# Expert tiles taken in pairs: the last 48 hidden columns of two tiles turned together and multiplied on half of the array's rows each, with their weights fetched per tile

## The chip, the cores and the metric

The kernel runs on one core of one Trainium2 chip, as one launch. The time is the device time of that core in microseconds (us), taken as a median over runs; a profile is one execution of its own. Engines are named as the profile does: PE multiplies matrices (PEld is its loading of weights), DVE is the vector engine, ACT the scalar engine, POOL is GpSimd, and SP issues most transfers. Each engine works through its own list of instructions in order, and waits where one needs a result that is not there.

## The reference, cut to what matters

The input is x, 4 sequences of 1024 rows with 256 columns, all in float32. Four blocks follow, each added to x: an attention, a mixture of experts, a short convolution, and the same mixture of experts once more. The two mixtures are what the change is about:

```
shared_out = silu_and_mul(xf @ shared_w1.T) @ shared_w2.T      # hidden width 352
probs      = softmax(xf @ gate_w.T);  weights, selected = top_k(probs, 6)   # 16 experts
gate_up    = einsum('th,eoh->teo', xf, w1)                      # 2 x 176 columns per expert
act        = silu(gate) * up                                    # 176 columns
moe_out    = einsum('te,tei,ehi->th', combine, act, w2)         # 176 -> 256
```

The kernel computes only the six chosen experts of each row. An expert's hidden width is 176: one block of 128 and a rest of 48.

## The kernel before

All of x stays in on-chip memory as X. The 4096 rows are split in two groups of 2048 (16 blocks of 128 rows each). A mixture of experts over one group is a *stage*, so there are four: group 0 and group 1 of the first mixture, then group 0 and group 1 of the second. Rows are sorted by expert in DRAM: POOL scatters each normalized row to six slots of a queue `xq` (96 scatters of 128 rows each per stage, `scatter`, L397), the stage works through the queue in 111 tiles of 128 slots, all slots of a tile having one expert, writes the results to `yq`, and POOL gathers them back (96 gathers per stage, `combine`, L1121), where DVE adds them into X with their routing weight (L1131, one for each gather).

`stream` (L986) runs all 4 x 111 = 444 tiles in rounds. Round c issues, in this order on each engine:

- `load`: every third round, SP reads the rows of three tiles, six tiles ahead (L1001).
- `gate_up(c)` (L1018): PE loads the expert's number into a register and multiplies the turned rows by 352 columns of `wgu`, which holds the weights of all experts; ACT takes the silu and DVE multiplies (L1039) into `hbuf`.
- `turn_h(c-2)` (L1041): two PE transposes of the 256 columns of `hbuf` (176 are filled, the rest is zero), one ACT copy. DVE's product of a tile is thus needed two rounds later.
- `turn(c+2)`: two PE transposes of the input rows, one ACT copy.
- `down(c-3)` (L1049): the 128 rows `w2a`, then the rest `w2b`, padded with zeros to 128 rows; both hold all experts. ACT copies the result to `yo`; SP writes `yo` to `yq` for three tiles at once.
- the *callback* of tile c-3: one call of `bites.step`.

A float32 multiplication is two passes, so it shows as two PE instructions; a transpose shows as one.

The callbacks fit all other work between the tiles. It lies in three lanes of generators, cut by `yield` into pieces ("bites"), and `bites.step(pe, (q, s, f))` issues up to q, s and f bites of the lanes QUEUE, SIDE and FILL, of these at most `pe` with PE work. In the two middle stages (L1202):

- QUEUE first holds the gathers of the stage before (48 bites of two gathers; each bite also uses the gathers of an earlier bite, which DVE waits for), and later the scatters for the next stage (one bite of preparation, 48 of two scatters).
- SIDE: whenever the gathers have completed a quarter of the group (12 bites), a convolution (9 bites, nearly all DVE) and a preparation of the routing (6 bites: statistics, root on ACT, normalizing on DVE, then three with PE work, the first of which turns the normalized rows, tile `fpt`) are added. After the last quarter comes `plan` (14 bites, mostly DVE), which sorts the rows. The scatters are added to QUEUE once SIDE is empty.
- FILL: the shared expert (`shared`, L930), one bite after every fourth tile.

If the scatters are not all issued when round 109 of a stage needs the first row of the next, `force` issues the rest there, and PE waits for them (`turn`). The first stage (`first`) has QUEUE scatters for stage 1 only, the last one (`final`) only gathers. After the last tile there remain the gathers of group 1, with the shared expert of group 1 between them.

The order on PE, DVE, ACT and SP is exactly that of the program.

Of the kernel before, what the change touches and what calls it, by code (L numbers as in the profile page):

```python
# [15 lines left out]
PE = mybir.EngineType.PE  # L16

# [20 lines left out]
FB = FI - P  # L38
VW = D + 1
# [64 lines left out]
def block_kernel(  # L104
# [193 lines left out]
    def plan(g, ps):  # L298
# [80 lines left out]
        for c in range(0, NTILE, 37):  # L379
            yield "el"  # L380
            le = rt.tile([1, 37, NEXP], FP, name="le")
            sh_le = [1, 37, NEXP]
            nc.vector.tensor_tensor(
                le,
                base[:, None, :].to_broadcast(sh_le),
                row0[:, c : c + 37, None].to_broadcast(sh_le),
                ALU.is_le,
            )
            nc.vector.tensor_reduce(ex[:, c : c + 37], le, AX.X, ALU.add)
# [498 lines left out]
    with ExitStack() as fctx:  # L888
# [3 lines left out]
        f3 = fctx.enter_context(tc.tile_pool(name="f3", bufs=3))  # L892
        ps_t = fctx.enter_context(tc.tile_pool(name="ps_t", bufs=2, space=PSUM))
        ps_g = fctx.enter_context(tc.tile_pool(name="ps_g", bufs=2, space=PSUM))
        ps_y = fctx.enter_context(tc.tile_pool(name="ps_y", bufs=1, space=PSUM))
        ps_s = fctx.enter_context(tc.tile_pool(name="ps_sh", bufs=2, space=PSUM))
        ps_m2 = fctx.enter_context(tc.tile_pool(name="ps_m2", bufs=1, space=PSUM))

        def ps_f():
            return ps_m2  # L900
# [14 lines left out]

        w2r = w2.rearrange("(n i) e -> i n e", i=FI)
        w2a = fw.tile([P, NEXP, E], FP, name="w2a")
        nc.scalar.dma_start(out=w2a, in_=w2r[0:P])
        w2b = fw.tile([P, NEXP, E], FP, name="w2b")
        nc.vector.memset(w2b[32:64], 0.0)  # L920
        nc.vector.memset(w2b[64:P], 0.0)
        nc.scalar.dma_start(out=w2b[0:FB], in_=w2r[P:FI])
        wgu_f = [wgu[:, k].rearrange("p n f -> p (n f)") for k in range(2)]
        w2_f = [w.rearrange("p n e -> p (n e)") for w in (w2a, w2b)]

        hbuf = [fw.tile([P, 2 * P], FP, name=f"hbuf{i}") for i in range(4)]
        for hb in hbuf:
            nc.vector.memset(hb[:, FI:], 0.0)

        def shared(g, i):  # L930
# [12 lines left out]
            for k in range(2):  # L943
                pt = ps_s.tile([P, 512], FP, tag="s", name="hpt")
# [3 lines left out]
            for s, rows in enumerate(S_ROWS):  # L948
                yield "pe"
                pg = ps_s.tile([P, 512], FP, tag="s", name="pg")  # L950
                pu = ps_s.tile([P, 512], FP, tag="s", name="pu")
# [14 lines left out]
            for pr in range(2):  # L966
                yield "pe"
                po = ps_s.tile([P, 2, E], FP, tag="s", name="po")
# [17 lines left out]
        def stream(stages):  # L986
# [5 lines left out]
            xg, xT, hT, yo, off = {}, {}, {}, {}, {}  # L992
# [24 lines left out]

            def gate_up(c):  # L1018
                st, i = tiles[c]
                _, vals = nc.values_load_multi_w_load_instructions(  # L1020
                    plan_of[st][2][0:1, i : i + 1],
                    engines=[PE],
                    min_val=0,
                    max_val=NEXP - 1,
                    skip_runtime_bounds_check_because="an expert's number",
                )
# [10 lines left out]
                h = hbuf[c % 4]  # L1037
                nc.scalar.activation(h[:, 0:FI], pg[:, 0:FI], AF.Silu)  # L1038
                nc.vector.tensor_mul(h[:, 0:FI], h[:, 0:FI], pg[:, FI:])  # L1039

            def turn_h(c):  # L1041
                pt = ps_t.tile([P, 2, P], FP, tag="t", name="pht")
                for k in range(2):
                    nc.tensor.transpose(pt[:, k, :], hbuf[c % 4][:, k * P : (k + 1) * P], ident)  # L1044
                hT[c] = f3.tile([P, 2, P], FP, name="hT")
                d = nc.scalar.copy(hT[c], pt)  # L1046
                pace["after"] = d.ins.name

            def down(c):  # L1049
                st, i = tiles[c]  # L1050
                py = ps_y.tile([P, E], FP, name="py")
                for k in range(2):
# [268 lines left out]
```

## Time and profile before

| what | us |
|---|---|
| median of 3 runs (lowest, highest) | 2390.59 (2389.18, 2391.22) |
| profiled execution, device time | 2393.24 |
| its span, first to last instruction | 2391.5 |
| PE busy | 2114.5 (88%) |
| DVE, ACT, POOL busy | 1118.5, 1240.2, 901.4 |
| attention, up to the first weights of the experts | about 765 |
| tiles of the four stages, with the waits between | 857 to 2260 |
| gathers and shared expert after the last tile | 2260 to 2391 |

The profile's page gives busy time per engine and 40 slices of the span; groups of instructions are named by line, engine and "out<-in"; a timeline merges instructions of one kind that follow each other (x4) and gives the start of the first. Starts are therefore what one measures with; the ends of PE's multiplications are modelled and overlap the next one's start.

### The profile page before, as it was taken

Reading aid. Unit: us, or ns where it says so; the run is one execution under the profiler, and the core shown is the slowest. Engines: PE = TensorE matmul, PEld = TensorE weight load, DVE = VectorE, ACT = ScalarE, POOL = GpSimd, SP = SyncE. Lnnn points to the kernel's source line nnn. Section 1 sums busy time; section 2 is a strip of 40 time slices with the busy share of each in tenths; the row PEclk is TensorE's granted clock in tenths of the full one; section 3 lists DMA queues with packets and bytes.
Section 4 is the critical chain, followed back from the end, with each engine's and each line's share of the span. In section 5 each row is a group of like instructions: output and inputs, shape, how many; then the busy total and the mean of one; then the engine's idle time right before and its main releaser. Section 6 shows DMA issues by size and latency. Waiting matters only on the chain.

```text
span 2391.5 us, 33033 instructions
## 1 busy us (share of the span) xinstructions
PE 2114.5 (88%) x10480; PEld 1308.4 (55%) x10480; DVE 1118.5 (47%) x2532; ACT 1240.2 (52%) x2754; POOL 901.4 (38%) x990
## 2 busy tenths in 40 slices
PE   5899999778898998999899999789999959999974
PEld 2344443222233466777666667567676747777632
DVE  5888867656555225111166652126754212441154
ACT  3677878566676145555455544335553424555410
POOL 3333211344431000444355226645513654540176
PEclk8888988889888999999999999989999979999987
DMA  7900000111101412555455335344423535663243
GB/s 232 342 7 1 1 1 1 38 51 45 53 27 62 114 48 79 165 166 166 137 151 154 102 104 176 132 139 142 145 92 121 176 124 154 202 186 115 91 123 112
DMA packets 212231, 267.73 MB, mean 112 GB/s; under 512 B 25280, under 2 KB 187232, under 8 KB 212064
## 3 DMA queue, kind: packets, MB, share of 16 engines
q1 hardware_dynamic: 166944, 161.04, 21.6%
q0 software_dynamic: 36992, 100.78, 13.4%
q10 hardware_dynamic: 8128, 3.80, 0.7%
q8 instruction: 91, 1.49, 0.3%
q14 instruction: 76, 0.62, 0.1%
HBM read 123.72 MB, written 141.82 MB: 111 GB/s over the span
## 4 chain that ended last, share of the span: by engine, by line
PE 67%; DVE 12%; issue 7%; ACT 7%; POOL 5%; DMA 2%; ACTq 0%; POOLq 0%; DVEq 0%; SPq 0%
PE pgu L1030 20%; PE py L1053 14%; PE ps L694 6%; PE acc L742 4%; PE pxt L1014 4%; PE pht L1044 4%; POOL xq L421 3%; PE pg L955 3%; ACT s L705 3%; PE pj L571 3%; PE pu L955 3%; PE po L972 3%; POOL yg L1147 2%; ACT s L863 1%; DVE X L1131 1%
## 5 line engine op out<-in xcount | busy, mean ns | idle before, releaser
L421 POOL DMA_INDIRECT xq<-sxn,sloti x384 | 379.2, 987 | 644.7 <-ACT xgT L1016 306.2
L1030 PE MATMUL pgu<-wgu,xgT 128*128 x1776 | 609.7, 466 | 4.4 <-DVE hbuf L1039 2.2
L1147 POOL DMA_INDIRECT yg<-yq,sloti x384 | 375.8, 979 | 421.8 <-issue 201.4
L1039 DVE TENSOR_TENSOR hbuf<-hbuf,pgu 128x176 f32<-128x176 f32 x444 | 149.4, 337 | 721.7 <-ACT hbuf L1038 721.2
L1030 PEld LDWEIGHTS pgu<-wgu,xgT 128*128 128x128 f32 x1776 | 338.7, 193 | 136.5 <-issue 20.3
L1038 ACT ACTIVATE hbuf<-pgu 128x176 f32<-128x176 f32 x444 | 141.4, 318 | 411.7 <-PE pgu L1030 411.6
L705 ACT ACTIVATE s<-ps 128x1024 f32<-128x1024 f32 (+3 forms) x384 | 291.4, 815 | 114.6 <-PE ps L694 113.5
L1053 PE MATMUL py<-w2a,hT 128*128 x888 | 268.7, 385 | 0.9 <-ACT yo L1062 0.9
L1053 PE MATMUL py<-w2b,hT 128*128 x888 | 266.4, 382 | 0.0
L1062 ACT COPY yo<-py 128x256 f32<-128x256 f32 x444 | 166.1, 374 | 167.0 <-PE py L1053 166.7
L1131 DVE SCALAR_TENSOR_TENSOR X<-yg,top,X 128x256 f32<-128x256 f32 x384 | 186.0, 484 | 87.8 <-DMA yg<-yq,sloti 81.8
L1014 PE MATMUL pxt<-ident,xg 128*128 128x128 f32 x888 | 171.8, 276 | 60.6 <-DMA xg<-xq 60.6
L714 POOL TENSOR_SCALAR_AFFINE_SELECT s<-s 128x256 f32<-128x256 f32 x128 | 84.2, 659 | 349.7 <-ACT s L705 349.5
L725 DVE TENSOR_TENSOR s<-s 128x1024 f32<-128x1024 f32 (+3 forms) x160 | 168.2, 1051 | 86.8 <-ACT s L705 83.5
L1016 ACT COPY xgT<-pxt 128x256 f32<-128x256 f32 x444 | 167.9, 378 | 68.7 <-PE pxt L1014 68.3
L694 PE MATMUL ps<-q,kA 32*128 32x512 f32 (+3 forms) x1024 | 182.0, 647 | 20.0 <-ACT s L705 18.0
L1044 PEld LDWEIGHTS pht<-ident,hbuf 128*128 128x128 f32 x888 | 125.9, 142 | 124.4 <-issue 71.1
L1053 PEld LDWEIGHTS py<-w2b,hT 128*128 128x128 f32 x888 | 170.2, 192 | 23.5
L863 ACT ACTIVATE s<-s 128x1024 f32<-128x1024 f32 x192 | 164.4, 856 | 27.5 <-POOL s L714 27.2
L1044 PE MATMUL pht<-ident,hbuf 128*128 128x128 f32 x888 | 171.6, 275 | 4.9 <-ACT hT L1046 4.9
L1046 ACT COPY hT<-pht 128x256 f32<-128x256 f32 x444 | 165.4, 372 | 1.7 <-PE pxt L1014 0.7
L742 PE MATMUL acc<-s,vA 128*32 128x512 f32 (+3 forms) x1024 | 140.1, 603 | 13.2 <-ACT s L863 10.8
(158 smaller groups left out, 2421.9 us busy)
## 6 DMA issues: line engine op xcount, KB each, us to landing
xg<-xq SPq DMA_DIRECT2D x148, 384.0 KB, 3.7
yq<-yo SPq DMA_DIRECT2D x148, 384.0 KB, 2.8
xq<-zero SPq DMA_DIRECT2D x74, 384.0 KB, 4.6
xq<-sxn,sloti POOLq DMA_INDIRECT x384, 2.4
yg<-yq,sloti POOLq DMA_INDIRECT x384, 2.9
wgu<-in_w SPq DMA_DIRECT2D x4, 1408.0 KB, 17.8
X<-in_x SPq DMA_DIRECT2D x8, 512.0 KB, 5.5
out<-X SPq DMA_DIRECT2D x8, 512.0 KB, 3.5
```

The lines of the kernel that those rows point to most:

```text
L421: d = nc.gpsimd.indirect_dma_start(out=xq[g][:, :], out_offset=bass.IndirectOffsetOnAxis(ap=sloti[:, c + i, k : k + 1], axis=0), in_=xs[:, ...
L694: nc.tensor.matmul(tiles[h // 2][:, h % 2, 0:nq], lhsT=kt[32 * h : 32 * h + 32, (j % 4) * P : (j % 4 + 1) * P], rhs=qT[u, hf][a][32 * h : ...
L705: nc.scalar.activation(s2[:, :, 0:nq], tiles[pr][:, :, 0:nq], AF.Square)
L725: nc.vector.tensor_mul(part, part, part)
L742: nc.tensor.matmul(acc[32 * r : 32 * r + 32, n0:512], lhsT=va[:, j % 4, h * VW : h * VW + 32], rhs=s2s[r // 2][:, r % 2, 0 : 512 - n0], st ...
L863: nc.scalar.activation(part, part, AF.Square)
L1014: nc.tensor.transpose(pt[:, k, :], xg[c][:, k * P : (k + 1) * P], ident)
L1030: nc.tensor.matmul(pg, lhsT=xT[c][:, k, :], rhs=wgu_f[k][:, bass.ds(vals[0] * (2 * FI), 2 * FI)], start=(k == 0), stop=(k == 1),)
L1044: nc.tensor.transpose(pt[:, k, :], hbuf[c % 4][:, k * P : (k + 1) * P], ident)
L1053: nc.tensor.matmul(py, lhsT=hT[c][:, k, :], rhs=w2_f[k][:, bass.ds(off[c] * E, E)], start=(k == 0), stop=(k == 1),)
L1131: nc.vector.scalar_tensor_tensor(X[:, t, l, :], yg[:, k, :], top[:, i, k0 + k : k0 + k + 1], X[:, t, l, :], op0=ALU.mult, op1=ALU.add,)
L1147: nc.gpsimd.indirect_dma_start(out=yg[:, k, :], out_offset=None, in_=yq[g][:, :], in_offset=bass.IndirectOffsetOnAxis(ap=sloti[:, i, k0 + ...
```

## The change

Tiles of a stage are taken in pairs (55 pairs and one single tile). The product of the even tile lies in the first 176 of 384 columns of an `hbuf`, that of the odd tile in the last 176; so the middle 128 columns hold the last 48 of the even tile, 32 zeros, and the first 48 of the odd one. `turn_h` turns the outer block of each tile, and the middle block once per pair. `down` runs once per pair: each tile's block of 128 against `w2a[0]` or `w2a[1]` (rows 0 to 127 and rows 48 to 175 of each expert), then the rest of each tile on 64 of the 128 rows of the array (rows 0 to 63 and 64 to 127), with 48 weight rows and 16 zero rows. These rest weights no longer lie on chip for all experts: in the round that turns a tile's input rows, two before its `gate_up`, SP loads the expert's number and fetches 48 KB into one of three buffers. Results are copied and written for two tiles at once.

The rest of the edit is in the fitting of other work: `plan` counts its table in pieces of 19, so in six bites where it had three; the middle stages take one and two bites of QUEUE in turn (they took one) and three of SIDE (they took two); the gathers of the last stage and after it come two to a bite, one bite after each tile, where they came three to a bite after every second tile; four gather buffers and three bites in flight where there were three and two; the shared expert and the preparation use one pool of two PSUM buffers, where the preparation had one of its own.

```diff
-        for c in range(0, NTILE, 37):
+        for c in range(0, NTILE, 19):
+            n = min(19, NTILE - c)
...
+        f4 = fctx.enter_context(tc.tile_pool(name="f4", bufs=4))
...
-        w2a = fw.tile([P, NEXP, E], FP, name="w2a")
-        nc.scalar.dma_start(out=w2a, in_=w2r[0:P])
-        w2b = fw.tile([P, NEXP, E], FP, name="w2b")
-        nc.vector.memset(w2b[32:64], 0.0)
-        nc.vector.memset(w2b[64:P], 0.0)
-        nc.scalar.dma_start(out=w2b[0:FB], in_=w2r[P:FI])
+        w2a = []
+        for a in range(2):
+            w2a.append(fw.tile([P, NEXP, E], FP, name=f"w2a{a}"))
+            nc.scalar.dma_start(out=w2a[a], in_=w2r[a * FB : a * FB + P])
+        w2b = [fw.tile([P, E], FP, name=f"w2b{i}") for i in range(3)]
+        for w in w2b:
+            nc.vector.memset(w, 0.0)
...
+            def fetch(c):
+                _, vals = expert(c, SP)
+                if tiles[c][1] % 2 == 0:
+                    rows, src = slice(0, FB), bass.ds(vals[0] * FI + P, FB)
+                else:
+                    rows, src = slice(P - FB, P), bass.ds(vals[0] * FI, FB)
+                nc.sync.dma_start(out=w2b[nth_pair(c) % 3][rows, :], in_=w2[src, :])
...
             def turn_h(c):
                 pt = ps_t.tile([P, 2, P], FP, tag="t", name="pht")
-                for k in range(2):
-                    nc.tensor.transpose(pt[:, k, :], hbuf[c % 4][:, k * P : (k + 1) * P], ident)
+                c0 = 2 * P * (tiles[c][1] % 2)
+                nc.tensor.transpose(pt[:, 0, :], pair(c)[:, c0 : c0 + P], ident)
+                if ends_pair(c):
+                    nc.tensor.transpose(pt[:, 1, :], pair(c)[:, P : 2 * P], ident)
...
             def down(c):
                 st, i = tiles[c]
-                py = ps_y.tile([P, E], FP, name="py")
-                for k in range(2):
-                    nc.tensor.matmul(
-                        py,
-                        lhsT=hT[c][:, k, :],
-                        rhs=w2_f[k][:, bass.ds(off[c] * E, E)],
-                        start=(k == 0),
-                        stop=(k == 1),
+                n = i % 2 + 1
+                py = ps_y.tile([P, 2, 512], FP, name="py")
+                for a in range(n):
+                    nc.tensor.matmul(
+                        py[:, a, 0:E],
+                        lhsT=hT[c + 1 - n + a][:, 0, :],
+                        rhs=w2a_f[a][:, bass.ds(off[c + 1 - n + a] * E, E)],
+                        start=True,
+                        stop=False,
                     )
...
+                for a in range(n):
+                    rows = slice(HP * a, HP * a + HP)
+                    nc.tensor.matmul(
+                        py[:, a, 0:E],
+                        lhsT=hT[c][rows, 1, :],
+                        rhs=w2b[nth_pair(c) % 3][rows, :],
+                        start=False,
+                        stop=True,
                     )
...
                 if c >= 3:
-                    down(c - 3)
+                    if ends_pair(c - 3):
+                        down(c - 3)
+                if c + 2 < n:
+                    fetch(c + 2)
...
-                    yg = f3.tile([P, n, E], FP, tag="yg", name="yg")
+                    yg = f4.tile([P, n, E], FP, tag="yg", name="yg")
...
-                    if len(pending) > 2:
+                    if len(pending) > 3:
                         use()
...
-                bites.step(1, (1, 2, 0))
+                bites.step(1, (1 + i % 2, 3, 0))
...
-                bites.add(QUEUE, combine(0, 3, store))
-            bites.step(1, (1 if i % 2 == 0 else 0, 0, 0))
+                bites.add(QUEUE, combine(0, 2, store))
+            bites.step(1, (1, 0, 0))
...
-            bites.add(QUEUE, combine(1, 3, last))
+            bites.add(QUEUE, combine(1, 2, last))
```

## The prediction

> **What bounds the kernel now.** I read the page's 40 slices and the shares of the chain that ended last, then timelines of PE, POOL and DVE inside a middle stage.
>
> ```profile
> PE   5899999778898998999899999789999959999974
> POOL 3333211344431000444355226645513654540176
> PE 67%; DVE 12%; issue 7%; ACT 7%; POOL 5%; DMA 2%; ACTq 0%; POOLq 0%; DVEq 0%; SPq 0%
> ```
>
> From slice 14 on (857 us) PE is full but for dents at slices 26 and 33, the boundaries of stages, and the end. A plain tile:
>
> ```profile
> 1208.04 1.35 PE L1030 MATMUL pgu<-wgu,xgT 128*128 x4
> 1209.22 0.38 PE L1044 MATMUL pht<-ident,hbuf 128*128 128x128 f32 x2
> 1209.44 0.38 PE L1014 MATMUL pxt<-ident,xg 128*128 128x128 f32 x2
> 1209.66 0.60 PE L1053 MATMUL py<-w2a,hT 128*128 x2
> 1210.09 0.59 PE L1053 MATMUL py<-w2b,hT 128*128 x2
> 1210.52 1.35 PE L1030 MATMUL pgu<-wgu,xgT 128*128 x4
> ```
>
> Start to start: four passes of 352 columns 1.18 us, a transpose 0.11, a pass of 256 columns 0.216; 2.48 in all, nothing between them. What PE saves here counts, unless something else must keep up with it. At a boundary it didn't:
>
> ```profile
> 1538.38 0.38 PE L1044 MATMUL pht<-ident,hbuf 128*128 128x128 f32 x2
> 1564.44 0.66 PE L1014 MATMUL pxt<-ident,xg 128*128 128x128 f32 x2 [25.68 <-DMA xg<-xq]
> 1540.00:1567.00 27.00, 2.56 (x7) 2.18 (x8) 0.00 (x0) 0.53 (x2) 14.89 (x16) 0.55 0.31 107
> ```
>
> PE waits for the next stage's rows while POOL (fifth pair) issues 16 last scatters. There are three such waits, 9.5, 25.8 and 25.8 us.
>
> **Change, 1: the pair's rest on PE.** Gone per pair: one transpose (0.109). The rest's four passes were 4 x 0.2165 = 0.866. They become four passes on 64 rows. The trace has no such tiling; the nearest row is the attention's on 32 rows, with the same 256 columns:
>
> ```profile
> 674.67 0.66 PE L182 MATMUL pt<-ident,at 128*128 128x128 f32 x4
> 675.25 0.71 PE L694 MATMUL ps<-q,kB 32*128 32x256 f32 x8
> 675.90 0.70 PE L794 MATMUL pw<-wout_sb,aT 128*128 128x256 f32 x2
> ```
>
> Eight passes take 0.65 instead of 8 x 0.216 = 1.73, so different row groups do run together. But the switch costs: in the single records the first pass starts 0.095 late after the last full-array one, then its weights stand open for 0.107, the way back costs 0.091 (both in the 0.65), and the first full-array weights after it 0.107 more. So the rest is 0.095 + 0.65 + 0.107 = 0.85: as dear as before. Net 0.016 + 0.109 = 0.125 per pair, x220 pairs = -28 us; four single tiles switch for nothing, +1.7. **-26 us**; a tile falls from 2.488 to 2.425. Bounds: switches free, 0.40 more per pair; no overlap, 0.43 less.
>
> The Trainium skill, TensorEngine Tiling (Array Packing), section Theoretical Speedup, gives "Up to 2×" for a dimension of 64 or less: the rest would fall to 0.43 and the pair save 0.54, 119 us in all. Its section Key Properties warns that changing the tiling mode drains the engine, without a price; the rows above hold the price, and the sum goes by them.
>
> **2: fetches.** SP gains per tile one register load (0.3 on PE, which does the same), one issue (0.36) and half a store instead of a third. About 1.0 us of a 2.4 us tile; bound 0. Behind SP's wait for the pair's copy stand the next fetch and rows. A fetch is issued four or more tiles (9.7 us) before `down` needs it; the 384 KB rows land in 3.7. Without that cover each pair would pay the difference. ACT's longer copies lie beside PE.
>
> **3: boundaries.** I counted bites by the program's own rule. Before: 3, 16 and 16 scatters are left, as the row shows (x16). After: `plan` has three more bites and `first` the same rates, so 6 are left at the first boundary (+3 x 1.27 = +3.8); in the middle stages the scatters end with tile 77 of 111, so two waits go: -51.6. **-47.8.** What is late next is point 4.
>
> **4: keeping up with the faster bites.** POOL runs flat out:
>
> ```profile
> 1180.53 0.99 POOL L1147 DMA_INDIRECT yg<-yq,sloti  x1 [22.25 <-DMA yq<-yo]
> 1181.82 0.98 POOL L1147 DMA_INDIRECT yg<-yq,sloti  x1 [0.30 <-issue]
> 1183.10 0.94 POOL L1147 DMA_INDIRECT yg<-yq,sloti  x1 [0.31 <-issue]
> 1184.35 0.94 POOL L1147 DMA_INDIRECT yg<-yq,sloti  x1 [0.30 <-issue]
> ```
>
> A gather each 1.253 us: 2.5 per tile before, like PE's 2.49; three per tile now ask 3.76 of a 2.43 us tile. DVE uses them in order, the tile's own product stands behind, and PE needs that two rounds later. Harder still is the convolution and preparation, after which PE must turn `fpt`. DVE's rows of one such chain (start is what counts):
>
> ```profile
> 1260.93 1.40 DVE L190 BATCH_NORM_STATS2 ln_st<-X 128x6 f32<-128x256 f32 x4
> 1266.17 1.52 DVE L200 TENSOR_SCALAR hn<-X,c_mv,c_rstd 128x256 f32<-128x256 f32 x4
> 1267.73 1.23 DVE L1111 TENSOR_TENSOR y<-hn,kb 128x1024 f32<-128x1024 f32 x1
> 1277.89 1.22 DVE L1119 TENSOR_TENSOR X<-X,y 128x1024 f32<-128x1024 f32 x1
> 1283.55 1.52 DVE L200 TENSOR_SCALAR rxn<-X,mvs,rstds 128x256 f32<-128x256 f32 x4
> ```
>
> Before, 24 us over six tiles, PE's own work there 17.5; it waited 4.5 in that quarter. After, the same bites fall into four tiles. DVE's serial sum: statistics 1.67, root 0.4, normalizing 1.77, shared product 0.6; products and sums of the next tile 4.45; of the third 0.86, silu 1.2, sum 1.25; preparation 1.6 + 0.4 + 1.75; eight gathers used at 0.455, three tile products at 0.25: 20.3 us. PE's own meanwhile, four tiles and a shared bite of 3.45: 13.15. (The same sum for the quarter above gives a wait of 3.7, measured 4.5.) Per middle stage, counted from the callback of its first tile:
>
> - first quarter: POOL starts at 1.6, gather 24 is issued 23 x 1.253 later, lands 2.9 later and is used (0.5): 33.8, plus 20.3 = 54.1; PE's own to `fpt` 35.9. Wait 18.2.
> - second: the chain starts 1.2 after PE ends the tile: 1.2 + 20.3 - 13.15 = 8.4. Third, with a shared bite of 2.6: 9.2. Fourth, without gathers, 1.2 + 16.1 - 10.6 = 6.7.
> - `plan`: from the last logits DVE's list to `mask` is 23.1 - 10.1 = 13 us over two tiles: 8.2 (before 5.1).
> - scatters at 1.267, 3.8 us per tile: the last normalized rows need 72 scatters done: 19.7 (DVE's list after `plan`'s product) + 91.2 + landing 2.4 + 0.8 = 114; PE's own to there, 32 tiles and its shared bites, 103. Wait 11.
>
> Sum 61.7, against 13.2 of waits over 0.5 us inside a stage before: +48.5, twice, **+97**. Bounds: below, DVE never idle between quarters (30 us each) and no wait for scatters: 31.6, so +37 for both; above, PE's clock after each long wait (0.55 in the row at the boundary), some 1.5 x 6 per stage, +18, against 5 saved at the old boundaries.
>
> **5: the rest.** ACT's first copies no longer wait for zeroing `w2b` (8.9 us on ACT), but the shared weights land 4.8 after 767.4 anyway: -1 (0 to -4). The last stage's gathers ask 2.51 per tile against 2.43, with two rounds in hand: 0 (to +4). The last 96 gathers run at POOL's pace before and after (2264 + 96 x 1.253 = 2384): 0.
>
> **Sum**: -26 - 47.8 + 97 - 1 = +22. On the profiled execution: span 2391.5 to 2413.5, time 2393.2 to 2415; it stands 2.65 above the median 2390.59, from which I forecast **2412 us**, 0.9% slower.
>
> **Rivals.**
> - *The faster bites cost little*: DVE is kept busy through the quarters and only its work counts (31.6 per stage): 2412 - 2 x 30 = 2352, faster. For it: PE is given slack of two rounds and DVE is 47% busy. Against: `fpt` follows the normalizing by one round only. It decides the sign from 51 us of waits per middle stage downwards.
> - *Switching is cheaper on 64 rows*: free, 0.2 less per tile; the first and last stages gain 22 and 14, the middle ones 10 each, where about 51 tiles aren't bound by DVE or POOL: 2356; at half the price 2383. Against: four different ways into a tiled mode all cost 0.095.
> - *The halves don't overlap* (the change doesn't do what it says): 0.216 more per tile, in the same tiles, 24 + 24 + 2 x 11: 2482. Against: the attention's overlap.
> - *Fetches are late*: over a 9.7 us lead, each further us on 220 pairs +220. Nothing speaks for it.
>
> **How the numbers follow.** Forecast 0.51 (2390 to 2440, by point 4's size), cheap bites 0.22, cheaper switch 0.16, no overlap 0.06, others 0.05. The range 2352 to 2440 cuts the lower half of the first rival and what is above the clock's bound. A difference under 0.2% can't be told here. Faster: 0.22, most of the third's 0.16 and the forecast's lowest edge: 0.35; within 0.2%: 0.07; slower: 0.58.
>
> **What the profile after would show.** Right: no wait for `xg` at the second and third boundary, about 13 at the first; waits of PE at `fpt` of 18, 8, 9, 7 us per middle stage, behind DVE; plain tiles of the first stage at 2.43; the two halves' first passes starting within 0.02 us, 0.20 after the previous pass; scatters 1.27 apart from about tile 45 to 80. Wrong: pairs well under 4.8 us, or quarters of a middle stage under 32 us, would make it faster.

## The result, and the profile after

The changed kernel takes 2425.92 us (median of 4 runs, 2425.29 to 2427.14) against 2390.90 for the kernel before: a ratio of 1.0147, 95% interval 1.0130 to 1.0165. The forecast was 2412 us, slower, within 2352 to 2440. The profiled execution has a span of 2424.3 us against 2391.5: 32.8 us to be explained, where the prediction's sum said 22.

The page's slices and the shares of the chain that ended last, for the changed kernel:

```profile
PE   5898999777788999999788899997889999999980
POOL 2333211443531000444476077037507604720166
PE 56%; DVE 13%; issue 8%; POOL 8%; ACT 7%; DMA 6%; ACTq 0%; SPq 0%; POOLq 0%; DVEq 0%
```

The two deep dents of PE at the ends of the middle stages are gone. In their place PE runs at 7 and 8 tenths through the first half of each middle stage (slices 19 to 22 and 27 to 29, counted from 0), and PE's share of the chain falls from 67% to 56%, while DVE, POOL and DMA hold more of it. POOL has an empty slice in the middle of the stage (22, where all gathers are issued and the plan isn't ready) and one at its end (25, where all scatters are).

To see where the time went, I cut both traces at PE's first product of each stage:

| part | before, us | after, us | difference | the prediction's sum |
|---|---|---|---|---|
| up to the first stage (attention, routing) | 854.8 | 869.7 | +14.9 | -1 |
| first stage | 314.1 | 307.2 | -6.9 | -3 |
| second stage | 401.9 | 413.1 | +11.2 | +16 |
| third stage | 406.2 | 418.0 | +11.8 | +16 |
| last stage, 110 tiles | 275.8 | 272.1 | -3.7 | -7 |
| from there to the end | 138.7 | 144.2 | +5.5 | 0 |

Busy times in three stretches of the second stage, cut at its tiles 50 and 80, show what happened within a middle stage. The columns are the stretch, its length, busy time of PE, PEld, DVE, ACT and POOL, then PE's granted clock, the share of DMA and GB/s. Before:

```profile
1168.90:1342.00 173.10, 165.08 (x761) 119.34 (x761) 102.31 (x260) 92.44 (x237) 94.49 (x94) 0.99 0.51 150
1342.00:1446.10 104.10, 98.86 (x445) 72.09 (x444) 54.44 (x161) 52.06 (x137) 21.35 (x22) 0.97 0.32 101
1446.10:1570.80 124.70, 99.02 (x441) 73.07 (x441) 19.70 (x51) 43.17 (x129) 73.17 (x76) 0.89 0.44 146
```

After:

```profile
1176.90:1394.60 217.70, 182.60 (x762) 114.58 (x761) 142.26 (x383) 95.17 (x223) 99.45 (x96) 0.89 0.44 132
1394.60:1495.50 100.90, 92.36 (x404) 58.68 (x403) 19.50 (x54) 37.10 (x111) 76.58 (x80) 0.97 0.59 190
1495.50:1590.00 94.50, 94.50 (x431) 61.51 (x429) 16.23 (x42) 38.32 (x116) 15.67 (x17) 1.00 0.41 130
```

The third stretch is 30.2 us shorter: POOL's scatters (73 us of busy POOL) have moved into the second one, and the boundary's wait is gone. The first stretch is 44.6 us longer. POOL does the same gathers there (94.5 and 99.5 us busy), but DVE has 142 us of work in it instead of 102: the convolutions, preparations and the plan now all fall into the first 50 tiles. And PE is granted 0.89 of its clock there instead of 0.99. In the records of the granted clock, PE has half speed for 47.8 us of this stretch, and for 3.4 us before.

Some of its waits, in the changed kernel's timeline of PE, with the lists of ACT and DVE beside it:

```profile
1226.98 0.48 PE L1077 MATMUL pht<-ident,hbuf 128*128 128x128 f32 x1 [5.35 <-ACT hT L1082]
1227.74 1.92 PE L1091 MATMUL py<-w2a,hT 128*128 x4
1230.46 1.45 PE L1062 MATMUL pgu<-wgu,xgT 128*128 x4
...
1233.09 1.45 PE L1062 MATMUL pgu<-wgu,xgT 128*128 x4 [0.74 <-DVE hbuf L1071]
1237.42 0.48 PE L1077 MATMUL pht<-ident,hbuf 128*128 128x128 f32 x1 [2.88 <-ACT hT L1082]
1241.96 1.44 PE L184 MATMUL fpt<-ident,rxn 128*128 128x128 f32 x4 [0.71 <-DVE rxn L202]
```

```profile
1224.24 0.30 ACT L197 ACTIVATE c_rstd<-c_mv,eps_t 128x4 f32<-128x4 f32 x1 [7.09 <-DVE c_mv L194]
...
1226.55 0.38 ACT L1082 COPY hT<-pht 128x256 f32<-128x256 f32 x1
...
1235.84 1.06 ACT L1162 ACTIVATE y<-y 128x1024 f32<-128x1024 f32 x1 [4.64 <-DVE y L1160]
...
1237.00 0.36 ACT L1082 COPY hT<-pht 128x256 f32<-128x256 f32 x1
```

```profile
1222.13 0.48 DVE L1176 SCALAR_TENSOR_TENSOR X<-yg,top,X 128x256 f32<-128x256 f32 x1 [0.60 <-DMA yg<-yq,sloti]
1222.53 1.40 DVE L192 BATCH_NORM_STATS2 ln_st<-X 128x6 f32<-128x256 f32 x4
1224.79 1.56 DVE L202 TENSOR_SCALAR hn<-X,c_mv,c_rstd 128x256 f32<-128x256 f32 x4
1227.09 0.33 DVE L1071 TENSOR_TENSOR hbuf<-hbuf,pgu 128x176 f32<-128x176 f32 x1
...
1232.70 0.33 DVE L1071 TENSOR_TENSOR hbuf<-hbuf,pgu 128x176 f32<-128x176 f32 x1
```

DVE uses the quarter's last gather at 1222.13 and only then can it take the convolution's statistics. ACT waits 7.09 us for them, to take their root (`c_rstd`). The copy that PE's transposes wait for (`hT`, 1226.55, by the releaser in PE's row) stands behind that root in ACT's list, so PE waits 5.35 us. Ten microseconds later the same happens with the convolution's silu (`y`): ACT waits 4.64 us for DVE, and PE 2.88 for the copy behind it. The tiles' own products on DVE (`hbuf`, 1227.09 and 1232.70) are late too, but only the wait of 0.74 us is put down to one. After such a wait PE's passes are slow: the four against `w2a` take 1.92 us in the row above, 1.03 in a plain pair.

A plain pair of the first stage has no other work in it:

```profile
986.59 0.70 PE L1100 MATMUL py<-w2b,hT 64*128 64x256 f32 x4
987.23 1.45 PE L1062 MATMUL pgu<-wgu,xgT 128*128 x4
988.51 0.27 PE L1077 MATMUL pht<-ident,hbuf 128*128 128x128 f32 x1
988.62 0.27 PE L1079 MATMUL pht<-ident,hbuf 128*128 128x128 f32 x1
988.73 0.38 PE L1044 MATMUL pxt<-ident,xg 128*128 128x128 f32 x2
988.95 1.35 PE L1062 MATMUL pgu<-wgu,xgT 128*128 x4
990.14 0.27 PE L1077 MATMUL pht<-ident,hbuf 128*128 128x128 f32 x1
990.25 0.38 PE L1044 MATMUL pxt<-ident,xg 128*128 128x128 f32 x2
990.46 1.03 PE L1091 MATMUL py<-w2a,hT 128*128 x4
991.42 0.70 PE L1100 MATMUL py<-w2b,hT 64*128 64x256 f32 x4
```

From one rest to the next it is 4.83 us, three transposes of `hbuf` instead of four. Of the three boundary waits one is left, the first. The kernel before has 9.31 us there:

```profile
1163.36 0.66 PE L1014 MATMUL pxt<-ident,xg 128*128 128x128 f32 x2 [9.31 <-DMA xg<-xq]
```

```profile
1157.64 0.27 PE L1079 MATMUL pht<-ident,hbuf 128*128 128x128 f32 x1
1171.46 0.66 PE L1044 MATMUL pxt<-ident,xg 128*128 128x128 f32 x2 [13.55 <-DMA xg<-xq]
```

In the text, boundary waits are counted from start to start less the pass's own length, which gives some 0.2 us more than these rows.

### The profile page after: what moved, and what is told of

It reads as the page before. It is cut to its first block, busy times and chain, and to the rows that moved or that the text cites. A ratio compares the mean times of both kernels' runs of the same rounds, so it can differ in the third digit from the quotient of the medians.

```text
span 2424.3 us, 34170 instructions
## 1 busy us (share of the span) xinstructions
PE 2103.5 (87%) x10260; PEld 1175.1 (48%) x10260; DVE 1114.5 (46%) x2556; ACT 1169.8 (48%) x2534; POOL 905.9 (37%) x990
## 4 chain that ended last, share of the span: by engine, by line
PE 56%; DVE 13%; issue 8%; POOL 8%; ACT 7%; DMA 6%; ACTq 0%; SPq 0%; POOLq 0%; DVEq 0%
PE pgu L1062 18%; PE py L1091 5%; POOL xq L424 5%; PE ps L697 4%; PE py L1100 4%; DMA yg<-yq,sloti 4%; PE pg L961 3%; PE po L978 3%; PE acc L745 3%; POOL yg L1192 3%; PE pxt L1044 3%; PE pu L961 3%; ACT s L708 3%; DVE X L1176 2%; DMA xq<-sxn,sloti 2%
## 5 line engine op out<-in xcount | busy, mean ns | idle before, releaser
L1062 PE MATMUL pgu<-wgu,xgT 128*128 x1776 | 632.5, 479 | 30.1 <-DVE hbuf L1071 28.5
L1192 POOL DMA_INDIRECT yg<-yq,sloti x384 | 382.6, 996 | 495.7 <-issue 228.7
L1062 PEld LDWEIGHTS pgu<-wgu,xgT 128*128 128x128 f32 x1776 | 311.3, 194 | 200.2 <-issue 59.2
L1108 ACT COPY yo<-py 128x512 f32<-128x512 f32 x224 | 130.9, 584 | 242.6 <-PE py L1100 242.6
L1091 PE MATMUL py<-w2a,hT 128*128 x888 | 236.5, 390 | 0.8 <-ACT yo L1108 0.7
L866 ACT ACTIVATE s<-s 128x1024 f32<-128x1024 f32 x192 | 164.4, 856 | 47.8 <-POOL s L717 47.7
L1044 PE MATMUL pxt<-ident,xg 128*128 128x128 f32 x888 | 173.5, 278 | 13.5 <-DMA xg<-xq 13.5
L1100 PE MATMUL py<-w2b,hT 64*128 64x256 f32 x888 | 162.3, 440 | 5.8 <-DMA w2b<-in_w 5.8
L1091 PEld LDWEIGHTS py<-w2a,hT 128*128 128x128 f32 x888 | 155.4, 195 | 13.9 <-ACT yo L1108 1.5
L1077 PE MATMUL pht<-ident,hbuf 128*128 128x128 f32 x444 | 124.0, 279 | 34.8 <-ACT hT L1082 34.8
L1082 ACT COPY hT<-pht 128x128 f32<-128x128 f32 (+1 forms) x444 | 140.5, 317 | 2.0 <-PE pht L1079 1.0
L1044 PEld LDWEIGHTS pxt<-ident,xg 128*128 128x128 f32 x888 | 112.3, 143 | 48.2 <-issue 45.9
```

Of the source, the lines that this page charges most:

```text
L1044: nc.tensor.transpose(pt[:, k, :], xg[c][:, k * P : (k + 1) * P], ident)
L1062: nc.tensor.matmul(pg, lhsT=xT[c][:, k, :], rhs=wgu_f[k][:, bass.ds(vals[0] * (2 * FI), 2 * FI)], start=(k == 0), stop=(k == 1),)
L1091: nc.tensor.matmul(py[:, a, 0:E], lhsT=hT[c + 1 - n + a][:, 0, :], rhs=w2a_f[a][:, bass.ds(off[c + 1 - n + a] * E, E)], start=True, stop=F ...
L1100: nc.tensor.matmul(py[:, a, 0:E], lhsT=hT[c][rows, 1, :], rhs=w2b[nth_pair(c) % 3][rows, :], start=False, stop=True,)
L1192: nc.gpsimd.indirect_dma_start(out=yg[:, k, :], out_offset=None, in_=yq[g][:, :], in_offset=bass.IndirectOffsetOnAxis(ap=sloti[:, i, k0 + ...
```

## The experiments

The first four ran together on one chip, on which the kernel before took 2390.61 us, as beside the result; it is called the first chip here. The other eight ran on three other chips, on each of which the kernel before took 2476 to 2479 us; there I read ratios to it and stretches of the traces. The changed kernel itself was not run on those.

### The plan's three extra bites alone

```diff
-        for c in range(0, NTILE, 37):
+        for c in range(0, NTILE, 19):
+            n = min(19, NTILE - c)
```

> The kernel before, with one edit: the table of plan counted in six pieces of 19, so plan has three bites more; no pairs, old rates. My theory: these three bites alone moved the scatters of the attention against its masks and cost the 15 us that the profile after shows before the first expert tile (start at 869.7 instead of 854.8); and they leave 6, 20 and 20 scatters at the boundaries (3, 16, 16), +3.8 + 5.1 + 5.1. So 2391 + 15 + 14 = 2420, expert tiles beginning at about 870. Rival: the 15 us come from something else in the changed kernel (placement in memory, the run): 2405, tiles from about 855.

Measured: 2425.51 us, ratio 1.0135 (1.0116 to 1.0153). The smallest edit of the change, three more places in a list of bites, costs as much as the whole. The first stage starts at 870.6 us instead of 854.8, and the boundary waits are 13.3, 30.7 and 30.9 us instead of 9.5, 25.8 and 25.8. What ACT waited for in the attention's last part (540 to 790 us), POOL's masks alone, is in this answer for the kernel before, the kernel with the three bites, and the changed kernel:

```profile
ACT s L863 <- POOL s L714: 9.0, 3, 4.9
```

```profile
ACT s L864 <- POOL s L715: 26.0, 5, 6.1
```

```profile
ACT s L866 <- POOL s L717: 25.9, 5, 6.1
```

The plan of the first group is handed out during the attention, ahead of the scatters. With three bites more, POOL's scatters, 12 in a row at 1.27 us each, stand at other places of the attention, and the masks behind them on POOL come late for ACT: 17 us more, in the kernel with this one edit and in the changed kernel alike. The attention's +14.9 is thus not of the pairs, the fetches or the pools. The figure is known to some 4 us: in the next run, whose attention has no edit either, the first stage starts at 850.8 us. Of the 35 us of this run some 16 are the attention's; the rest lies in the first three stages, in their longer boundary waits above all.

### The faster bites alone

```diff
-                bites.step(1, (1, 2, 0))
+                bites.step(1, (1 + i % 2, 3, 0))
```

> The kernel before, with one edit: the middle stages take one and two bites of QUEUE in turn and three of SIDE; no pairs, three gather buffers as before. The scatters then end with tile 76, so two waits of 25.8 go. My theory: the waits that the profile after shows inside a middle stage (13.9, 5.5, 5.9, 3.5 us for the quarters, 8.4 for plan, 8.3 for the scatters) appear here too, a little smaller since PE's own tiles are longer: +28 to +33 per stage. 2391 - 51.6 - 5 + 60 = 2395, between 2385 and 2405: about the same as before. By the sum on record (61.7 per stage) it would be 2434. Rival (they cost little): 2391 - 57 = 2335.

Measured: 2428.55 us, ratio 1.0158 (1.0138 to 1.0179). The expectation is missed by 34 us; the record's point 4 gave 2434. This kernel has no pairs, yet its second stage shows the changed kernel's picture:

```profile
1164.90:1389.80 224.90, 187.04 (x789) 129.56 (x788) 141.09 (x378) 102.02 (x249) 97.32 (x97) 0.89 0.39 116
1389.80:1490.20 100.40, 93.66 (x418) 67.80 (x417) 18.89 (x53) 41.78 (x125) 76.21 (x80) 0.98 0.55 180
1490.20:1586.30 96.10, 96.10 (x442) 71.25 (x442) 15.89 (x41) 42.97 (x129) 15.02 (x16) 1.00 0.34 108
```

First stretch +51.8 us against the kernel before, last stretch -28.6, the same 0.89 of the clock, 47.8 us at half speed. The middle stages are 19.5 and 16.3 us longer although 25.8 us of waiting left each: the faster bites cost 45 and 42 us inside a stage, more than they save at its end. The next run asks what they do together with the pairs.

### The change with the old rates

```diff
-                bites.step(1, (1 + i % 2, 3, 0))
+                bites.step(1, (1, 2, 0))
```

> The changed kernel, with the middle stages' old rates, one bite of QUEUE and two of SIDE per tile. By the count of bites 22 scatters (16 before) are then left at the second and third boundary: waits of 22 x 1.27 + 5.7 = 33.6 us each instead of none. My theory: the faster bites cost about as much inside the stages as they save at the boundaries: waits inside fall from about 46 (waits over 0.8 us in the profile after) to the 13 of before, so 2426 + 2 x (33.6 - 33) = 2427, between 2415 and 2440. Rival (the faster bites pay): waits inside don't fall, 2426 + 67 = 2493.

Measured: 2439.81 us (2431.48 to 2443.25), ratio 1.0207 (1.0190 to 1.0224), at the upper edge of the expectation. The boundary waits are back, and longer than in the kernel before (13.5, 33.3 and 33.9 us), since the pairs get through their tiles sooner and the plan is three bites longer. Beside the pairs and the longer plan, then, the faster bites are worth some 14 us by the medians; without them they cost 38. The two boundary waits that they remove are 67 us here instead of 52, which explains 15 us of that difference. The traces add that the faster bites cost 29 and 32 us inside a middle stage here, and 45 and 42 without pairs; why less, these runs do not say.

Set beside the kernel with the plan's bites alone, which has the same rates and the same plan, this run shows what the rest of the change does: 2439.81 against 2425.51, so the pairs, the fetches and the gathers' new bites and buffers cost 14 us together (4 in the two profiled executions). They save 11.2 us in the first stage and 3.5 in the last one's 110 tiles, and lose 6.7 in each middle stage and 3.5 after the last tile. So what each part of the change costs depends on what it is added to.

### The rest on all rows of the array

```diff
-                    rows = slice(HP * a, HP * a + HP)
...
-                        lhsT=hT[c][rows, 1, :],
-                        rhs=w2b[nth_pair(c) % 3][rows, :],
+                        lhsT=hT[c][:, 1, :],
+                        rhs=w2b[nth_pair(c) % 3],
```

The pair's two rests are multiplied one after the other on all 128 rows, without a switch and without overlap. Each tile thereby also adds the other tile's rest to its result.

> The changed kernel, with the rest of each tile multiplied on all 128 rows of the array and the pair's whole 128 weight rows; so nothing is switched and nothing runs together. Each tile then gets the other tile's rest added, so the result is not the reference's; number and length of the passes are the same. My theory, from the profile after: a pair's rest with its switch takes about as long (entry 0.096, weights 0.107, two steps of 0.214, way back 0.093, weights 0.107: 0.83 us) as four passes in a row (0.866), so +0.04 us x 220 pairs less 4 x 0.4 for the single tiles: +6 us where PE is the bound, 2429 to 2432. Rival: the overlap of the halves is worth its 0.43 us per pair: some +50 to +90, 2475 or more.

Measured: 2430.75 us, ratio 1.0173 (1.0156 to 1.0190), as the theory said. In the last stage's tiles 66 to 110, where PE has nothing else to do and waits for nothing, 44 tiles take 109.2 us before, 106.8 in this kernel and 106.0 in the changed one. A pair of this kernel, from rest to rest 4.86 us:

```profile
2221.40 1.03 PE L1099 MATMUL py<-w2b,hT 128*128 128x256 f32 x4
2222.26 1.35 PE L1062 MATMUL pgu<-wgu,xgT 128*128 x4
...
2225.39 1.03 PE L1091 MATMUL py<-w2a,hT 128*128 x4
2226.26 1.03 PE L1099 MATMUL py<-w2b,hT 128*128 128x256 f32 x4
2227.12 1.35 PE L1062 MATMUL pgu<-wgu,xgT 128*128 x4
```

The saved transpose explains 2.4 of the 3.1 us (22 pairs x 0.109); the two halves at the same time bring the other 0.7, or 0.03 us per pair. By that, half of the array for each tile is worth some 7 us in the kernel (an estimate: 220 pairs at 0.03); the medians differ by 4.8, about the spread of the runs.

### Three bites of the plan in the changed kernel

```diff
-            yield "el"
+            if c % 38 == 0:
+                yield "el"
```

> The changed kernel, with its six smaller pieces of the plan's table handed out two to a bite, so that the plan has three bites of it as in the kernel before. Theory (the three extra bites of the plan push each later bite of the attention by three places, so that scatters on POOL meet the diagonal masks, which cost the attention 15 us, and they leave three more scatters at the first boundary): the first stage starts at about 855 us of the span instead of 870, the first boundary's wait falls from 13.7 to about 9.5 us, no boundary waits after it, and the kernel takes 2407 us (2401 to 2413). Rival (the attention's 15 us come with the fetches or with the changed pools, not with the number of bites): the first stage starts at 866 us or later, and the time stays at 2420 to 2426 us.

> The changed kernel with three bites of the plan's table instead of six, once more, since the first four-kernel comparison with it was made on a chip on which the kernel before took 2479 us and whose traces show stretches in which every queue's plain steps took 0.7 us instead of 0.03. Theory: against a kernel before at 2391 us, the first stage starts at about 855 us, the first boundary's wait is about 9.5 us, and the time is 2407 us (2401 to 2413). Rival (the number of bites has no part in the attention's 15 us): 2420 to 2426 us. If the kernel before is far from 2391 us here too, the expectations hold as differences: 16 us above the kernel before, or 30 to 35.

Measured on two of the other chips: 2605.13 and 2591.07 us, ratios 1.0513 (1.0479 to 1.0547) and 1.0460 (1.0419 to 1.0502). The times fit neither theory: on these chips paired kernels are slow wherever gathers run, as the next part shows, and why stays open. The places do fit: the first stage starts at 858.2 and 855.8 us (878.6 in the six-bite kernel run beside it), the first boundary waits 10.0 and 9.5 us, and no other boundary waits. Of the attention's and the first boundary's share, then, the extra bites are the cause in the paired kernel too; what that is worth in time on the first chip, some 19 us, was not measured.

### Slow gathers, fast scatters

```diff
-            bites.step(1, (2 if i % 8 == 0 else 1, 2, 0))
+            bites.step(1, (2 if i % 5 == 0 else 1, 2, 0))
...
-                bites.step(1, (1, 2, 0))
+                bites.step(1, (1 + (i > 60 and i % 3 == 0), 2, 0))
```

In the kernel before, twice; and the same rates in the changed kernel, with three bites of the plan, twice (the run named after_split_tail is the same kernel as after_split).

> The kernel before, without pairs, with two changed rates: in the first expert stage every fifth tile (instead of every eighth) hands out a second bite of the gathering lane, and in the two middle stages the gathering lane keeps its one bite per tile until tile 60, after which every third tile hands out two. The gathers are then as slow as before, only the scatters at the end are faster. Theory (what the faster bites of the changed kernel cost is cost of the faster gathers and their followers, in the first 60 tiles; scatters can go faster at no price): all three boundary waits go (9.5 + 25.8 + 25.8 = 61 us), of which some 5 us come back among the scatters, so about 2335 us (2322 to 2350). Rival (each boundary wait only moves into the stage, because the scatters themselves hold up TensorE wherever they run): 2380 us or more.

> The kernel before, without pairs, with the faster scatters late in each stage (first stage: every fifth tile a second bite; middle stages: a second bite at every third tile from tile 60), once more for the same reason. On the disturbed chip the boundary waits went as foreseen (2.3, none, none), but waits of 1 to 4.5 us stood among the late scatters. Theory: with undisturbed queues those waits are mostly the disturbance, so 2335 us (2322 to 2360), 55 us below the kernel before. Rival (the boundary wait moves into the stage): 2380 us or more, no more than 10 us below the kernel before.

> The changed kernel with three bites of the plan's table and with the same two rates as the unpaired kernel beside it (first stage: every fifth tile two bites of the gathering lane; middle stages: one per tile until tile 60, then two at every third). Theory (the pairs themselves are worth 0.07 us of each of some 360 tiles, the rest of the change was rates): about 20 to 26 us below the unpaired kernel with the same rates, so 2310 us (2295 to 2330). Rival (the run with the whole rows shows that the pairs are worth no more than 5 us, since TensorE's gaps between the smaller products are filled less well by the rest of the work): within 8 us of the unpaired kernel.

> The changed kernel with three bites of the plan's table and the same two rates as the unpaired kernel beside it. Theory (the pairs are worth 26 us by the first record, 5 us by the run on whole rows; the plan's three bites and the late scatters give the rest): 2325 us (2305 to 2350), 5 to 26 us below the unpaired kernel with the same rates. Rival (the smaller pieces of work, and stores after each pair, leave TensorE more gaps than the pairs save): level with the unpaired kernel or above it.

Measured without pairs: ratios 0.9968 (0.9949 to 0.9988) and 0.9951 (0.9931 to 0.9970) to the kernel before, so 8 and 13 us faster instead of 55. It is the only version that beat the kernel before. The waits did leave the boundaries (2.3, 0 and 0 us), but in the second stage the tiles 66 to 110 with their scatters take 168 to 174 us, where the kernel before, on the first chip, took 165.5 with its wait of 25.8 in it. That fits the rival: the boundary's wait moved in among the scatters. The last experiment's kernel, with the old rates and boundary waits of 25.7 us, takes 175 us for these tiles on a third of the slower chips, so little was gained there. How much of that is those chips, I can't tell without the kernel before's trace there.

Measured with pairs: 2514.72 and 2504.43 us, ratios 1.0155 (1.0118 to 1.0192) and 1.0102 (1.0059 to 1.0145), 41 to 43 us above the unpaired kernel instead of 5 to 26 below. On these chips the paired kernel loses in stretches with gathers: the last stage's first 50 tiles take 165 to 170 us, and 134 to 136 in the unpaired kernel; on the first chip both take 127. The last stage's tiles 66 to 110 take 106.0 and 109.1 us on every chip. What ACT waits for in the last stage's first 50 tiles of this kernel (the second run):

```profile
ACT yo L1109 <- PE py L1101: 20.9, 13, 2.5
ACT hbuf L1071 <- PE pgu L1063: 18.5, 18, 3.4
ACT yo L1109 <- remote: 13.8, 3, 6.0
ACT hbuf L1071 <- issue: 12.0, 15, 2.0
```

Three times it waits up to 6 us for a buffer of `yo` whose store has not been reported back ("remote": a releaser that the trace does not show). On the first chip's trace of the changed kernel there is no such wait. All traces from these chips also hold only half of the landings of transfers that the first chip's hold, and those of kernels with fetches show stretches of 4 to 7 us in which SP's register and semaphore steps take 0.7 us instead of 0.02 to 0.06; whether the recording or the chip is behind it, these runs do not say.

### Two bites of the side lane

```diff
-                bites.step(1, (1 + i % 2, 3, 0))
+                bites.step(1, (1 + i % 2, 2, 0))
```

> The changed kernel with its middle step handing out two bites of the side lane per tile, as before, instead of three; the gathering lane keeps its one and a half. Theory (the waits within a middle stage are those on the gathered rows' followers: the side lane, at two bites per tile, is still emptied before the next gathers land, so its rate matters little): the same to within 8 us, 2418 to 2430 us, no boundary waits beyond the first. Rival (three side bites per tile crowd ACT and DVE and make the waits): the waits inside each middle stage fall by 15 us or more, and the kernel takes 2400 us or less.

Measured on another chip: 2608.01 us, ratio 1.0521 (1.0486 to 1.0555). The changed kernel wasn't run there, so this does not test the theory by time. Against the three-bite kernel beside it, the first 50 tiles of its middle stages take 238 and 242 us against 244, and the whole stages 473.5 and 477.6 against 482.2 and 481.7: no sign that the side lane's rate is what makes the waits.

### Fetched weights without pairs

```diff
+                nc.sync.dma_start(
+                    out=w2b[c % 6][0:FB, :], in_=w2[bass.ds(vals[0] * FI + P, FB), :]
+                )
...
-                        rhs=w2_f[k][:, bass.ds(off[c] * E, E)],
+                        rhs=w2b[c % 6] if k else w2a_f[:, bass.ds(off[c] * E, E)],
```

> The kernel before, without pairs and with its own rates, but with the 48 rows of each tile's down weights fetched per tile as in the changed kernel (a register load and a transfer of 48 KB on SP for each of 444 tiles, six buffers, fetched two tiles ahead; the resident copy goes). Theory (the record's second step: the fetches cost nothing but a short wait at each start of a stage, 1.4 to 3.1 us in the changed kernel): 3 to 10 us above the kernel before; the tiles without any other work (the last stage from its tile 66 on) stay at 2.48 us each. On a chip where the kernel before takes 2477 us instead of 2391, the changed kernel's last stage took 165 us for its first 50 tiles against 134 without pairs: the theory says that this comes of the fetches' records and register loads on SP, so that stretch takes 150 us or more there and the kernel 2530 to 2590 us. Rival (it comes of the gathers by twos and of a store for each pair): the stretch stays at 133 to 137 us and the kernel within 12 us of the kernel before. A third way (late fetches hold TensorE in every gathering stretch, on any chip): waits of the second product on the fetched rows of over 10 us in a stage, and 30 us or more above the kernel before.

Measured on a third of the other chips: 2495.13 us, ratio 1.0085 (1.0059 to 1.0110): the fetches cost some 19 us there, nearer the rival's 12 than the theory's 54. The last stage's first 50 tiles take 134.3 us, the rival's value; the next 16 take 46.5, where the unpaired kernels without fetches have 39.8. In those first 50 tiles 4 of SP's register and semaphore steps take over 0.5 us; in the paired kernels on these chips it is 18 to 24. So the 30 to 36 us that paired kernels lose in that stretch do not come of the fetches alone. They may come of the gathers by twos, of a store for each pair, or of these and the fetches together; that was not separated. No wait of PE in this trace is put down to fetched rows, and the time is below the 30 us of the third way, which falls.

## Why the prediction was right, point by point

The sign and the time (2412 against 2425.92) were right, by a sum in which four errors partly cancel (pairs, middle stages, attention, end). That they do is luck.

**1, the pair's rest: mechanism right, gain a little low.** Predicted 0.125 us per pair and -26 us; the plain stretch gives 3.1 us for 22 pairs, 0.14 per pair, some -31. In the single records the prices taken from the attention's 32 rows hold on 64: the first pass 0.096 late, the weights open for 0.107, the way back 0.092, the first full weights after it 0.107; the two halves' first passes start 7 ns apart. So neither "switching is cheaper" nor "the halves don't overlap" came true. The Trainium skill, TensorEngine Tiling (Array Packing), section Theoretical Speedup, lets one hope for "Up to 2×" on 64 rows. The run on all rows shows 0.03 us per pair for the halves, where half of 0.866 would be 0.43: with two products of 256 columns per visit, the 0.40 us of the way there and back (its Key Properties mention a drain) take nearly all of the gain.

**2, fetches at nothing: nearly right on this chip.** PE waits for fetched rows only at the stage starts (1.4, 3.1 and 1.5 us). On another chip the fetches alone cost 0.85%, which the record had no price for.

**3, boundaries: right.** Predicted 13.3 us at the first and none at the others; 13.7 and none. -47.4 against -47.8. (The middle stages' scatters run later than foreseen, while tiles 50 to 86 are multiplied, not 45 to 80.)

**4, keeping up with the faster bites: the sum right, the place of the waits wrong.** Predicted +48.5 per middle stage. Measured: the stage is 11.2 and 11.8 us longer, 25.8 left the boundary and the pairs give 7.9 (111 tiles at 0.071), so +44.9 and +45.5. The chain that the record priced is there. From POOL's first gather to PE's first `fpt` of a middle stage it takes 52.8 and 52.1 us, by the record 52.5; from the use of a quarter's last gather to its `fpt` it takes 19.8, 19.9, 19.4 and 16.1 us in the second stage, by the record 20.3 three times and 16.1.

But PE waits less in these chains than the record said, and elsewhere. The second stage's waits over 0.8 us, from start to start, are 46 us, not 61.7: the first quarter 13.9, with 1.4 for fetched weights in it (18.2), then 5.5, 5.9 and 3.5 (8.4, 9.2, 6.7), the plan 8.4 (8.2), the scatters 8.3 (11). Only 4.7 us of them stand at `fpt`, where the record put the quarters' 18, 8, 9 and 7. The transposes of `hbuf` have 17.4, behind ACT's copies, and `pgu` 14.6, behind DVE's products. The record counted ACT's root and silu as steps of DVE's list, but not that the copies that PE needs next stand behind them in ACT's list.

The rest of the 45 is what the record had put only into its upper bound: passes at half clock after the waits, 48 us of half speed instead of 3 in the first 50 tiles. There the waits over 0.8 us account for 30 of the 48 us (44.6 and the pairs' 3.5), so 18 are left; about 3 of these are PE's work for the fourth preparation and the plan, which came later before. PE works during 38.3 of the 47.8 us at half speed (3.0 before), so slow passes can have lost up to 18 us. The Trainium skill, TensorE: Matmul & The Clock Gate, section HAM oscillation, prices a cold stretch (one at half clock) as its length times (1 - 1.2/2.4). For 47.8 us that is an estimate of 24; the trace leaves less, since PE also stands waiting while its clock is down. Its "no PE-idle gaps >~3.4µs" is the milder rule: the wait of 2.88 us shown above left the next passes at half speed too.

The first rival, faster bites at little cost, is excluded by the run with the rates alone.

**5, the rest: the step that failed.** It listed ACT's first copies and the ends, and took the attention for untouched. The plan's three extra bites were counted for the first boundary (point 3) but not for the attention, where the same generator runs: +14.9 us instead of -1. And the last 96 gathers, which the record let run at POOL's pace before and after, did not: 119.8 us became 126.1. A bite of the shared expert now follows every two of these gathers, where it followed three. DVE waits for the shared expert's products (33.8 us between 2270 and 2390; 1.6 before), and six times POOL waits over a microsecond for a buffer:

```profile
2337.32 0.94 POOL L1192 DMA_INDIRECT yg<-yq,sloti  x1 [1.14 <-DVE X L1176]
2340.76 0.94 POOL L1192 DMA_INDIRECT yg<-yq,sloti  x1 [1.24 <-DVE X L1176]
2344.18 0.94 POOL L1192 DMA_INDIRECT yg<-yq,sloti  x1 [1.23 <-DVE X L1176]
```

That the shared expert's bites, now spread over fewer gathers, are the cause is read from the trace and wasn't tried.

The sum again, with what was measured: -31 for the pairs, -47 at the boundaries, +90 in the middle stages, +15 in the attention, +5.5 at the end: +32.5, against 32.8 found. That it closes proves little: the +90 is what remains of the middle stages after the other terms, and the -31 is the plain stretch's gain times 220. The last stage's first 50 tiles, with gathers, gain nothing (126.9 and 126.7 us), the first stage's gain more than 0.07 each (151.0 and 143.4).

## What to carry to other kernels

Where one generator is handed out in bites at several places, an extra bite is not free anywhere it runs: follow it through every user, since three bites of it cost 35 us of a kernel, some 16 of them in the attention, where scatters on POOL now delay masks that ACT waits for. Price a change's own gain in a stretch that has nothing else in it, and its side effects by cutting both traces at the same instructions of each stage; the pairs gain 0.07 us per tile there, and all else comes of what runs beside them. A wait that was removed by pulling work forward was paid for where the work went, and a wait of several microseconds can cost PE more than its length. When a chain runs through two engines, follow the lists of both: what PE waited for stood on ACT, behind ACT's own wait for DVE.

## What the runs showed of the hardware

- With waits of up to 7.5 us a few tiles apart, PE was granted half its clock for 47.8 of the 217.7 us of a middle stage's first 50 tiles, and just as long in the kernel without pairs; before, with four waits of 1.6 to 1.8 us and nothing longer there, for 3.4 us.
- Switching from 128 to 64 rows and back costs 0.40 us in all (0.096, 0.107, 0.092 and 0.107), about the same four prices as between 128 and 32 in the attention (0.095, 0.107, 0.091 and 0.107).
- The kernel before takes 2391 us on one chip and 2476 to 2479 on three others. In the parts that the unpaired kernels run there without an edit, the difference lies in the attention (+7 us), in stretches with gathers and in what follows the last tile; the last stage's plain tiles take 2.48 us on all. Paired kernels close to the changed one were 4.6 to 5.2% slower than the kernel before on two of those chips, where the change itself costs 1.5% on the first. A verdict on a kernel that leans on many small transfers may thus not carry from chip to chip.
